# Opening and closing turns of a 64-batch GNN and attention kernel: steps listed by hand, weights in 21 loads, and matmuls of zeros ahead of the first products

## The chip, the cores and the metric

The kernel runs on one core of a Trainium2 chip. A core has a matrix engine (TensorE, PE in the profile), a vector engine (VectorE, DVE), a scalar engine (ScalarE, ACT), a general engine (GpSimd, POOL) and a queue engine (SyncE, SP) that here only starts DMA transfers; sixteen DMA engines do the moving. Each engine works through its own instructions in the order in which they were written into its queue, and waits where one needs a result of another engine. The metric is the device time of one execution in microseconds (us); lower is better. A time is given as the median of the runs with the lowest and the highest.

## The reference

Two layers over 64 batches of 256 tokens with 512 features, all in float32. Layer 0 averages neighbours with a weighted adjacency matrix and applies one linear layer; layer 1 is attention of 8 heads whose scores are multiplied by twice the adjacency matrix. Both end in a residual and a normalisation.

```python
# layer 0
deg = jnp.sum(adj, axis=-1, keepdims=True)
agg = jnp.einsum('bij,bjf->bif', adj, x) / jnp.maximum(deg, EPS)
cat = jnp.concatenate([x, agg], axis=2)
out = jax.nn.relu(jnp.einsum('bnf,of->bno', cat, W))      # W is 512 x 1024
x = _layernorm(x + out, axis=-1)
# layer 1
q, k, v = proj(Wq, bq), proj(Wk, bk), proj(Wv, bv)        # each 512 x 512, 8 heads of 64
scores = jnp.einsum('bhqd,bhkd->bhqk', q, k) * SCALE
scores = scores * (adj + adj)[:, None, :, :]
attn = jax.nn.softmax(scores, axis=-1)
ctx = jnp.einsum('bhqk,bhkd->bhqd', attn, v)
x = _layernorm(x + (jnp.einsum('bse,fe->bsf', ctx, Wo) + bo), axis=-1)
```

## The kernel before

**Products.** Each of the four large products of a batch (L: layer 0 on x, 1024 columns; Q: queries and keys together; V; O: the output projection) is done as a two-by-two block product with seven multiplications in place of eight. So there are steps L1 to L7, Q1 to Q7, V1 to V7 and O1 to O7 (lines 320 to 356 and 370 to 417). The weights are kept as seven blocks: four that are loaded (B11, T3, B21, B22 before they are combined) and sums of them, T1 to T4, made by `sum_blocks` (line 171). The other operand has four sums as well: xS1 to xS4 from the turned x (`xT0`, `xT1`), yS from the turned layer-0 result (`x1T`), cS from the attention's context; they are made by POOL on line 288. Results leave PSUM by a copy (`Lk5`, `Qk4` and so on; ACT, for O on DVE) or by an addition to what is there (`Lj3`, `Vj2`; DVE, line 328).

**The other steps of a batch.** `Dzx` and `Dza` load x and adj in a form that DVE can turn (xT, aT), `Dx` and `Dadj` load them by rows. `AY0` and `AY1` multiply the adjacency with the layer-0 product (line 442), `AYa`, `AYb`, `AYp`, `AYn` add, normalise and write layer 0's result into x (ACT, line 434). `Dway` writes it to DRAM, `Dz1` reads it back turned by blocks, `x1T` finishes the turn on DVE (line 482). Then Q and V. `Sa` to `Sd` are the score products of four pairs of heads (line 517), `ma`.. the mask on DVE, `Ma`.. the row maxima, `ea`/`fa`.. the exponentials on ACT (line 546), `ra`.. reciprocals, `na`.. the scaling on ACT (line 563), `Ta`.. a turn on DVE (line 570), `Dwa` and `Dsa`.. a round trip through DRAM (lines 575 and 584). `C0a`, `C0b`, `C1a`, `C1b` multiply the attention of pairs a, b, c, d with v (line 600), `c0` and `c1` copy the context (ACT, line 616). `Drest` fetches layer 0's result again and `bo` adds the bias to it on POOL (line 496), O's keeping steps add it (line 415), `lb`, `lp`, `ln` normalise (lines 422 to 434) and `Dout` stores.

**Order.** The order on every queue is written by hand. `PLAN` lists each step once with an offset: a turn of the loop on line 660 takes steps of several batches, `Sa+0` of batch i, `L5+2` of batch i+2, `O1-1` of batch i-1. The loop runs i from -6 to B+5 (B is 64), and a step is left out where its batch does not exist. So the first and last turns are the plan with holes in it. Ahead of the loop stand the loads for the first batches and the weights: `first_weights` (line 179; W0 half on the SP queue, half on the ACT queue, then wq, the biases, and the turn and sums of batch 0), and `more_loads` (line 191; wk, wv, wo on SP). `load_blocks` issues one DMA for each block and each group of 32 partitions, 64 KB each, for wo one for each block: 84 in all. Inside the loop, `later_weights` (line 196) stands ahead of V2 of batch 0 and scales the query weights and sums wqk on DVE and wv on POOL in one piece; `last_weights` (line 203) stands ahead of `bo` of batch 0 and folds the value bias into the output bias with eight matmuls (`p_bv`, line 210).

**DMA issue.** The completion semaphores of the DMAs are eight, used in turn, so a queue issues its next DMA only when the one that used the same semaphore before has landed.

Of the kernel before, what the change touches and what calls it, by code (L numbers as in the profile page):

```python
# [7 lines left out]
F32 = mybir.dt.float32  # L8
AF = mybir.ActivationFunctionType
ALU = mybir.AluOpType  # L10
AX = mybir.AxisListType

P = 128
# [3 lines left out]

PLAN = """  # L20
    Sa+0 AYn1+1
    Sb+0 ma+0 ln0-2 Dway+1
# [34 lines left out]
    Q4+1 lb1-1 Vk4+1 lp0-1 AYn0+2 Qj3+1 lp1-1 AYb1+2  # L57
    Q2+1 Qk4+1 AYp1+2 ln1-1 Qj2+1
"""


@with_exitstack
def kernel(
# [12 lines left out]
    bo: bass.AP,  # L76
    out: bass.AP,
):

# [18 lines left out]
    nc = tc.nc  # L100
    B, N, F = x.shape
    H = 8
    D = F // H
    NT = N // P
    FC = F // P
    G = F // 2
    L = 32
    A = P // L
    R = 2 * NT

    QSCALE = 2.0 * D ** -0.5

    const = ctx.enter_context(tc.tile_pool(name="const", bufs=1))
# [15 lines left out]
    def bank(name, b):  # L129
        return tile_of(name, b, [P, F], banks, "ps")  # L130
# [12 lines left out]
    def groups():  # L143
        return ((a, slice(a * L, (a + 1) * L)) for a in range(A))
# [4 lines left out]

    B11, B21, B22, T1, T2, T3, T4 = range(7)
    w0 = const.tile([P, 7, 2, 2, G], F32, name="w0")
    wqk = const.tile([P, 7, 2, 2, G], F32, name="wqk")
    wv = const.tile([P, 7, 2, G], F32, name="wv")
    wo = const.tile([P, 7, 2, G], F32, name="wo")

    def load_blocks(queue, dst, dram, swapped=False, natural=False):

        for blk, kh, nh in ((B11, 0, 0), (T3, 0, 1), (B21, 1, 0), (B22, 1, 1)):  # L160
            nh ^= swapped
            cols = dram[:, nh * G : (nh + 1) * G]
            if natural:
                rows = cols.rearrange("(c p) o -> p c o", p=P)
                queue.dma_start(out=dst(slice(None), blk), in_=rows[:, 2 * kh : 2 * kh + 2])
                continue
            rows = cols.rearrange("(a c l) o -> a l c o", a=A, c=FC)
            for a, part in groups():
                queue.dma_start(out=dst(part, blk), in_=rows[a, :, 2 * kh : 2 * kh + 2])

    def sum_blocks(engine, w):
        for dst, a, b in ((T1, T3, B11), (T2, B22, T1), (T3, B22, T3), (T4, B21, T2)):
            engine.tensor_tensor(w[:, dst], w[:, a], w[:, b], ALU.subtract)  # L173

    bqk = const.tile([P, 2, FC], F32, name="bqk")
    bvT = const.tile([P, FC], F32, name="bvT")
    bo_sb = const.tile([P, F], F32, name="bo_sb")

    def first_weights():
        load_blocks(nc.scalar, lambda p, k: w0[p, k, :, 1], w0t[F:])  # L180
        load_blocks(nc.sync, lambda p, k: w0[p, k, :, 0], w0t[:F])
        load_blocks(nc.scalar, lambda p, k: wqk[p, k, :, 0], wqt, swapped=True)
        nc.scalar.dma_start(out=bqk[:, 0], in_=bq)
        nc.scalar.dma_start(out=bqk[:, 1], in_=bk)
        nc.scalar.dma_start(out=bvT, in_=bv.rearrange("o (c p) -> p (o c)", p=P))
        nc.scalar.dma_start(out=bo_sb, in_=bo.to_broadcast([P, F]))
        for name in ("xT0", "xT1", "xS1", "xS2", "xS4", "xS3"):
            run(name, 0)
        sum_blocks(nc.vector, w0.rearrange("p k c m o -> p k (c m o)"))

    def more_loads():
        load_blocks(nc.sync, lambda p, k: wqk[p, k, :, 1], wkt, swapped=True)
        load_blocks(nc.sync, lambda p, k: wv[p, k], wvt)
        load_blocks(nc.sync, lambda p, k: wo[p, k], wot, natural=True)

    def later_weights():
        nc.vector.tensor_scalar(bqk[:, 0], bqk[:, 0], QSCALE, None, ALU.mult)
        for k in (B11, T3, B21, B22):
            nc.vector.tensor_scalar(wqk[:, k, :, 0], wqk[:, k, :, 0], QSCALE, None, ALU.mult)
        sum_blocks(nc.vector, wqk.rearrange("p k c m o -> p k (c m o)"))  # L200
        sum_blocks(nc.gpsimd, wv.rearrange("p k c o -> p k (c o)"))

    def last_weights():

        bv_all = tile_of("bv_all", 0, [P, NT, F], tag="h1")[:, 0].rearrange("p (c q) -> p c q", c=FC)
        nc.vector.tensor_copy(bv_all, bvT.unsqueeze(2).to_broadcast([P, FC, P]))
        ps = bank("p_bv", 0)
        for n, blocks in enumerate(((B11, B21), (T3, B22))):
            for c in range(FC):
                nc.tensor.matmul(  # L210
                    ps[:, n * G : (n + 1) * G],
                    lhsT=bv_all[:, c],
                    rhs=wo[:, blocks[c // 2], c % 2],
                    start=(c == 0),
                    stop=(c == FC - 1),
                )
        nc.vector.tensor_tensor(bo_sb, ps, bo_sb, ALU.add)
        sum_blocks(nc.gpsimd, wo.rearrange("p k c o -> p k (c o)"))


    def turned_rows(dram, a, width):
# [83 lines left out]
    WEIGHTS = {1: B11, 2: B21, 3: B22, 4: T4, 5: T1, 6: T2, 7: T3}  # L305
# [38 lines left out]
    def right_weights(left, w, width):  # L344
        def multiply(k, b, ps, first):
            for c in range(2):
                nc.tensor.matmul(  # L347
                    ps[:, :width],
                    lhsT=left(k, b, c),
                    rhs=w[:, WEIGHTS[k], c],  # L350
                    start=first and c == 0,
                    stop=True,
                    skip_group_check=True,
                )

        return multiply
# [13 lines left out]
    def multiply_q(k, b, ps, first):  # L370
        for m in range(2):
            for j in range(2):
                for c in range(2):
                    nc.tensor.matmul(  # L374
                        ps.rearrange("p (m j q) -> p m j q", m=2, j=2)[:, m, j],
                        lhsT=wqk[:, WEIGHTS[k], c, m, j * P : (j + 1) * P],
                        rhs=left_y(k, b, c),
                        start=first and m == j == c == 0,
                        stop=True,
                        skip_group_check=True,  # L380
                    )
# [4 lines left out]
    def keep_q(b, ps, t, n):  # L386
        for m in range(2):
            for j in range(2):
# [6 lines left out]
                )  # L395

    winograd("Q", multiply_q, keep_q, part_q)

    def part_v(b, t, n):
# [239 lines left out]
            nc.sync.dma_start(out=token_rows(out[b], a), in_=held["h1", b][part])  # L639


    plan = [(name[:-2], int(name[-2:])) for name in PLAN.split()]
    done = set()

    def run(name, b):
        if 0 <= b < B and (name, b) not in done:
            done.add((name, b))
            steps[name](b)

    with tc.manual_schedule():  # L650
        run("Dzx", 0)
        first_weights()
        run("Dza", 0)
        run("Dadj", 0)
        run("Dx", 0)
        run("Dadj", 1)
        run("Dadj", 2)
        run("Dzx", 1)
        more_loads()
        for i in range(-6, B + 6):  # L660
            for name, ahead in plan:
                if name == "V2" and i + ahead == 0:
                    later_weights()
                if name == "bo" and i + ahead == 0:
                    last_weights()
                run(name, i + ahead)


# [34 lines left out]
```

## Time and profile before

| what | value |
|---|---|
| median of 3 runs | 3129.31 us (3128.94 to 3130.68) |
| time of the profiled execution | 3130.71 us |
| its span, first to last instruction | 3128.9 us |
| instructions | 51253 |
| PE busy | 3062.6 us |
| DVE, ACT, POOL busy | 2082.1, 1712.2, 974.2 us |
| DMA | 513.35 MB, mean 164 GB/s |
| mean granted TensorE clock | 0.992 |

The span leaves out 1.8 us of the profiled execution's own time, and the median of the other runs lies 0.4 us above the span. A group in the profile is one line of the program, one engine, one operation and the tiles it writes and reads; a row of the timeline gives start, length, engine, line, operation, written tile, read tiles, shape and count, and in brackets how long the engine stood idle before it and what ended that. `PEld` rows are the weight loads of the matrix engine, which run beside its multiplications. A float32 matmul appears as two rows of the count: L's step of two matmuls is `x4`.

### The profile page before, as it was taken

To read this page: it belongs to the slowest core of one execution; us is meant where nothing else is said; L and a number is where in the kernel's file an instruction comes from. 1 tells how busy PE (TensorE), PEld (TensorE's weight loads), DVE (VectorE), ACT (ScalarE), POOL (GpSimd) and SP (SyncE) were. 2 spreads that over 40 slices of the span, in tenths; PEclk is the share of its full clock that TensorE was granted. 3 is DMA by queue.
4 is the path that set the end of the run, shared out by engine and by line. 5 is a ranking of instruction groups with operands and counts; after the bars stand their busy time and mean duration, and the time that the engine had idled before them with its cause. 6 is when DMAs were issued, how large, how long until landed. Compare 5 with 4: busy or idle time off the path is not lost. (4 is left out here: it accounts for less than half of the span.)

```text
span 3128.9 us, 51253 instructions
## 1 busy us (share of the span) xinstructions
PE 3062.6 (98%) x17168; PEld 2265.9 (72%) x17168; DVE 2082.1 (67%) x3599; ACT 1712.2 (55%) x4993; POOL 974.2 (31%) x1677
## 2 busy tenths in 40 slices
PE   5999999999999999999999999999999999999996
PEld 2776777777777777777767777777777777777674
DVE  4666666666766766666666666667667666666664
ACT  1555556555555555555555565555555555555654
POOL 2233323323233233233333233232332332333332
PEclk8999999999999999999999999999999999999998
DMA  6565655656656656656666567566566566566555
GB/s 148 125 165 159 182 160 157 185 154 160 182 156 161 182 153 171 173 151 182 165 159 182 154 163 186 155 159 181 157 161 182 152 172 173 151 182 165 159 155 141
DMA packets 498183, 513.35 MB, mean 164 GB/s; under 512 B 114816, under 2 KB 399488, under 8 KB 497920
## 3 DMA queue, kind: packets, MB, share of 16 engines
q1 hardware_dynamic: 494400, 507.70, 60.5%
q8 instruction: 137, 2.24, 0.3%
q10 hardware_dynamic: 3520, 2.37, 0.3%
q14 instruction: 126, 1.03, 0.1%
HBM read 308.55 MB, written 201.33 MB: 163 GB/s over the span
## 5 line engine op out<-in xcount | busy, mean ns | idle before, releaser
L390 ACT ACTIVATE qk<-Qa,bqk 128x128 f32<-128x128 f32 x768 | 218.6, 367 | 241.2 <-PE Qa L374 241.2
L363 ACT COPY oy<-La 128x512 f32<-128x512 f32 x192 | 112.3, 585 | 433.2 <-PE La L347 433.1
L428 POOL TENSOR_SCALAR mv<-mv 128x1 f32<-128x1 f32 x256 | 55.7, 217 | 935.1 <-DVE mv L423 919.4
L405 ACT COPY v<-Va 128x256 f32<-128x256 f32 x192 | 70.1, 365 | 365.3 <-PE Va L347 365.3
L347 PE MATMUL Lc<-w,xS 128*128 128x512 f32 x512 | 249.8, 611 | 14.5 <-DVE w L173 14.5
L374 PEld LDWEIGHTS Qa<-x1T,wqk 128*128 128x128 f32 x2048 | 248.8, 192 | 6.6
L374 PEld LDWEIGHTS Qa<-yS,wqk 128*128 128x128 f32 x2048 | 248.8, 192 | 6.6
L288 POOL TENSOR_TENSOR cS<-cT 128x256 f32<-128x256 f32 x128 | 93.2, 729 | 509.2 <-ACT cT L616 509.2
L374 PE MATMUL Qc<-yS,wqk 128*128 128x128 f32 x2048 | 249.6, 275 | 0.0
L374 PE MATMUL Qa<-x1T,wqk 128*128 128x128 f32 x2048 | 249.3, 275 | 0.0
L374 PE MATMUL Qa<-yS,wqk 128*128 128x128 f32 x2048 | 249.3, 275 | 0.0
L347 PE MATMUL La<-w,xS 128*128 128x512 f32 x512 | 243.3, 598 | 5.4 <-POOL xS L288 3.0
L347 PE MATMUL La<-w,xT 128*128 128x512 f32 x512 | 241.6, 594 | 0.8 <-DVE oy L328 0.8
L374 PEld LDWEIGHTS Qc<-yS,wqk 128*128 128x128 f32 x2048 | 239.0, 192 | 0.0
L442 PE MATMUL AY<-oy,aT 128*128 128x512 f32 x512 | 233.0, 598 | 4.6 <-DVE oy L328 4.6
L415 DVE TENSOR_TENSOR h<-Oa,rest 128x256 f32<-128x256 f32 x192 | 81.5, 425 | 220.3 <-PE Oa L347 200.7
L328 DVE TENSOR_TENSOR oy<-Lc,oy 128x512 f32<-128x512 f32 x64 | 44.2, 691 | 276.0 <-PE Lc L347 271.0
L288 POOL TENSOR_TENSOR yS<-x1T 128x256 f32<-128x256 f32 x128 | 93.3, 729 | 350.2 <-DVE x1T L482 350.2
L347 PEld LDWEIGHTS Lc<-w,xS 128*128 128x128 f32 x512 | 93.2, 192 | 132.3 <-issue 108.8
L288 POOL TENSOR_TENSOR xS<-xT 128x256 f32<-128x256 f32 x128 | 93.4, 730 | 299.1 <-DVE xT L253 299.1
L454 DVE SCALAR_TENSOR_TENSOR oy<-AY,deg,oy 128x512 f32<-128x512 f32 x128 | 94.9, 741 | 135.7 <-PE AY L442 135.7
L546 ACT ACTIVATE sa<-sa,nmaxa 128x256 f32<-128x256 f32 x256 | 127.0, 497 | 99.8 <-DVE nmaxa L540 99.8
(119 smaller groups left out, 7274.4 us busy)
## 6 DMA issues: line engine op xcount, KB each, us to landing
zx<-in_x_dram SPq DMA_DIRECT2D x256, 128.0 KB, 3.6
x<-in_x_dram SPq DMA_DIRECT2D x256, 128.0 KB, 3.4
way<-x SPq DMA_DIRECT2D x64, 512.0 KB, 3.2
z<-way SPq DMA_DIRECT2D x256, 128.0 KB, 3.0
wsa<-sa SPq DMA_DIRECT2D x64, 512.0 KB, 2.6
wsb<-sb SPq DMA_DIRECT2D x64, 512.0 KB, 3.0
sTa<-wsa SPq DMA_DIRECT2D x256, 128.0 KB, 3.6
wsc<-sc SPq DMA_DIRECT2D x64, 512.0 KB, 2.7
```

What stands on the lines that cost most here:

```text
L288: nc.gpsimd.tensor_tensor(part_of(s, b, [P, 4, 2, P])[:, k], left(b), right(b), op)
L328: nc.vector.tensor_tensor(dst, ps.rearrange(shape, **sizes), dst, ALU.add)
L347: nc.tensor.matmul(ps[:, :width], lhsT=left(k, b, c), rhs=w[:, WEIGHTS[k], c], start=first and c == 0, stop=True, skip_group_check=True,)
L363: nc.scalar.copy(part_l(b, t, n), ps.rearrange("p (m o) -> p m o", m=2))
L374: nc.tensor.matmul(ps.rearrange("p (m j q) -> p m j q", m=2, j=2)[:, m, j], lhsT=wqk[:, WEIGHTS[k], c, m, j * P : (j + 1) * P], rhs=left_y ...
L390: nc.scalar.activation(part_q(b, t, n)[:, m, j], ps.rearrange("p (m j q) -> p m j q", m=2, j=2)[:, m, j], AF.Identity, bias=bqk[:, m, c : ...
L405: nc.scalar.copy(part_v(b, t, n), ps[:, :G])
L415: nc.vector.tensor_tensor(part_o(b, t, n), ps[:, :G], rest, ALU.add)
L428: nc.gpsimd.tensor_scalar(mv[:, 1:2], mv[:, 1:2], LN_EPS, None, ALU.add)
L442: nc.tensor.matmul(ps, lhsT=held["aT", b][:, j, t], rhs=held["oy", b][:, 1, j], start=(j == 0), stop=(j == NT - 1),)
L454: nc.vector.scalar_tensor_tensor(h, held[f"AY{t}", b], rdeg, h, ALU.mult, ALU.add)
L546: nc.scalar.activation(rows(b)[:, r], rows(b)[:, r], AF.Exp, bias=of("nmax", b)[:, r : r + 1], accum_out=of("total", b)[:, r : r + 1],)
```

## The change

`START` and `END` are two new lists with a batch behind each step. `START` replaces everything ahead of the loop and the loop's turns up to i = 2; the batch number is the true one. `END` replaces the turns from i = 60 on; its number counts from the end, 1 is batch 63. The loop keeps `PLAN` for i from 3 to 59. The guard against running a step twice is gone.

Weights are loaded whole: one DMA takes 32 partitions of all four blocks, 256 KB; wo is one DMA of 1 MB. That is 8 DMAs for W0, 8 for wq and wk, 4 for wv and 1 for wo, 21 in place of 84. The biases move from the ACT queue to the SP queue. A block is now a strided part of the loaded tile: the two halves (x part and neighbour part) of an L weight lie 2048 elements apart, where they were adjacent; the sums T1, T2, T4 have a tile of their own, T3 is formed in place. Each sum is a step of its own (`W0s1` to `W0s4`, and so on); those of wo stay on POOL, those of wv too. The scaling of the query weights (`WqS`) is one instruction on ACT, of 2048 elements a partition, in place of four on DVE of 512.

`warm` is new: DVE writes zeros into the place of the W0 sums, and PE multiplies them 12 times (128x512, float32).

```diff
+FIRST_TURN = 3
+LAST_TURNS = 4
+START = """
+    warm:0 Dzx:0 W0:0 xT1:0 xT0:0 xS1:0 xS3:0 Dx:0 xS2:0 Dza:0 xS4:0 Dadj:0 Dzx:1 L1:0 W0s1:0 W0s2:0 Dadj:1
+    L2:0 Lk1:0 W0s3:0 Wo:0 L6:0 W0s4:0 deg:0 L5:0 Lk6:0 aT:0 Wb:0 L7:0 Lk5:0 L3:0 Lj7:0 Dza:1 L4:0 Wq:0
+    Lj3:0 Lj2:0 Lk4:0 xT1:1 AY1:0 xT0:1 xS1:1 AY0:0 xS3:1 AYa1:0 L5:1 AYb1:0 AYa0:0 AYp1:0 L1:1 Dzx:2
+    xS2:1 AYn1:0 AYb0:0 L2:1 bv1:0 AYp0:0 aT:1 xS4:1 bv2:0 AYn0:0 Lk1:1 Dway:0 Wv:0 Lk5:1 Lj2:1 L6:1
+    Wos1:0 Lk6:1 WqS:0 L7:1 Dz1:0 L3:1 Lj7:1 Wqs1:0 Dx:1 L4:1 Lj3:1 Dadj:2 Wvs1:0 Wqs2:0 Lk4:1 Wos2:0
+    Dza:2 AY1:1 x1T:0 AY0:1 xT1:2 yS1:0 deg:1 yS2:0 Q1:0 Wqs4:0 Wvs3:0 AYa1:1 Wvs2:0 V1:0 Qk1:0 Q5:0
...
+"""
+END = """
...
+    Ok4:4 Sa:2 Dsb:3 ma:2 V5:2 fb:2 V1:2 Dsd:3 Ma:2 Vk5:2 V2:2 Vk1:2 lb1:4 fa:2 Sd:2 Drest:3 Dz1:1 md:2
...
+    c1:3 Mc:2 Q5:1 Qk1:1 yS2:1 Dwb:2 cS1:3 Q6:1 cS2:3 Qk5:1 cS3:3 fc:2 yS4:1 O1:3 cS4:3 Q3:1 Qk6:1 Ok1:3
+    Ta:2 yS3:1 ec:2 Q7:1 Qj3:1 Dwa:2 ed:2 rc:2 O6:3 Qj7:1 nc:2 Ok6:3 Sb:1 rd:2 mb:1 O7:3 nd:2 Sa:1 Dsa:2
+    Mb:1 O5:3 Tc:2 Q4:1 fb:1 Ok5:3 Dwc:2 Oj7:3 ma:1 Qk4:1 O4:3 Ma:1 eb:1 Q2:1 Td:2 ea:1 O2:3 Ok4:3 Dwd:2
+    Qj2:1 fa:1 C0a:2 Drest:2 Dsc:2 rb:1 Sc:1 nb:1 ra:1 Sd:1 Dsb:2 mc:1 O3:3 na:1 lb1:3 Dsd:2 Mc:1 lp1:3
+    Oj3:3 fc:1 Oj2:3 V1:1 lb0:3 ec:1 C1a:2 Ta:1 lp0:3 C0b:2 bo:2 ln1:3 md:1 Dwa:1 V5:1 ln0:3 rc:1 Md:1
+    C1b:2 nc:1 Dout:3 ed:1 Tc:1 fd:1 Tb:1 Dwc:1 Dsa:1 c0:2 rd:1 c1:2 Dwb:1 nd:1 O1:2 cS1:2 O2:2 cS2:2
+    Ok1:2 cS3:2 O6:2 Vk1:1 Td:1 Vk5:1 cS4:2 O5:2 Oj2:2 Dwd:1 V6:1 Ok6:2 Dsc:1 Ok5:2 O7:2 Vk6:1 V7:1
+    Dsb:1 Oj7:2 O4:2 O3:2 Ok4:2 lb1:2 Drest:1 V3:1 Dsd:1 Vj7:1 lp1:2 Oj3:2 V4:1 lb0:2 V2:1 Vk4:1 lp0:2
+    ln1:2 Vj2:1 Vj3:1 ln0:2 C0a:1 Dout:2 C1a:1 C0b:1 bo:1 C1b:1 c0:1 c1:1 O2:1 cS1:1 O1:1 cS2:1 O5:1
+    cS4:1 Ok1:1 O6:1 cS3:1 Ok5:1 O3:1 Ok6:1 Oj2:1 O7:1 Oj3:1 Oj7:1 lb0:1 O4:1 lp0:1 Ok4:1 lb1:1 ln0:1
+    lp1:1 ln1:1 Dout:1
+"""
...
+    def weights(name, engine, parts, flip=0):
+        raw = const.tile([P, parts, FC, 2, G], F32, name=name)
+        sums = const.tile([P, 3, parts, 2, G], F32, name=f"{name}_sums")
+        def block(k):
+            if k >= T1:
+                return sums[:, k - T1]
+            return raw[:, :, k // 2 * 2 : k // 2 * 2 + 2, k % 2 ^ flip]
...
+    def load_weights(queue, raw, part, dram):
+        rows = dram.rearrange("(a c l) (n o) -> a l c n o", a=A, c=FC, n=2)
+        for a, p in groups():
+            queue.dma_start(out=raw[p, part], in_=rows[a])
+    @step("W0")
+    def _(_):
+        load_weights(nc.scalar, w0_raw, 1, w0t[F:])
+        load_weights(nc.sync, w0_raw, 0, w0t[:F])
...
+    @step("WqS")
+    def _(_):
+        nc.scalar.mul(bqk[:, 0], bqk[:, 0], QSCALE)
+        nc.scalar.mul(wqk_raw[:, 0], wqk_raw[:, 0], QSCALE)
...
+    @step("warm")
+    def _(b):
+        zeros = w0(T1)[:, 0].rearrange("p c o -> p (c o)")
+        nc.vector.memset(zeros, 0.0)
+        ps = bank("p_warm", b)
+        for _ in range(12):
+            nc.tensor.matmul(ps, lhsT=zeros[:, :P], rhs=zeros, start=True, stop=True)
...
                 nc.tensor.matmul(
-                    ps[:, :width],
+                    ps[:, :width].rearrange("p (m o) -> p m o", o=G),
                     lhsT=left(k, b, c),
-                    rhs=w[:, WEIGHTS[k], c],
+                    rhs=w(WEIGHTS[k])[:, :, c],
...
-        for i in range(-6, B + 6):
-            for name, ahead in plan:
-                if name == "V2" and i + ahead == 0:
-                    later_weights()
-                if name == "bo" and i + ahead == 0:
-                    last_weights()
+        for name, b in listed(START):
+            run(name, b)
+        for i in range(FIRST_TURN, B - LAST_TURNS):
+            for name, ahead in turn:
                 run(name, i + ahead)
+        for name, b in listed(END):
+            run(name, B - b)
```

## The prediction

> **What bounds the kernel now.** I read the page's shares and slices first.
>
> ```profile
> PE 3062.6 (98%) x17168; PEld 2265.9 (72%) x17168; DVE 2082.1 (67%) x3599; ACT 1712.2 (55%) x4993; POOL 974.2 (31%) x1677
> ...
> PE   5999999999999999999999999999999999999996
> ...
> PEclk8999999999999999999999999999999999999998
> ```
>
> TensorE sets the time, and only the first and the last of 40 slices (78 us each) have holes. The steady turns leave nothing to win. PE's timeline gives the price of one, from the first context matmul of one batch to that of the next:
>
> ```profile
> 189.07 1.08 PE L600 MATMUL pc<-sTa,v 128*64 128x256 f32 x8
> ...
> 2991.37 1.08 PE L600 MATMUL pc<-sTa,v 128*64 128x256 f32 x8
> ...
> 3038.87 1.08 PE L600 MATMUL pc<-sTa,v 128*64 128x256 f32 x8
> ```
>
> The last two stand 47.50 us apart, and 189.07 to 3038.87 is 60 turns of 47.50. So 64 batches are 3040.0 us of matmuls, p_bv (148.70 to 152.15) 3.45 more: 3043.5 us. The span is 3128.9, so 85.4 us are lost. Where? Starts of neighbouring steps give 1.72 us for an L step and for each of AY0, AY1, 1.78 for a Q step, 0.865 for a V, O, S or C step; ahead of 189.07 stand batch 0, batches 1 and 2 each without C and O, L and AY of batch 3, and p_bv: 47.5 + 2 x 38.0 + 15.5 + 3.45 = 142.4 us. The start loses 46.7, the end the other 38.7. The waits of PE name most of it:
>
> ```profile
> PE Lc L347 <- DVE w L173: 14.5, 1, 14.5
> PE Vb L347 <- issue: 10.1, 1, 10.1
> PE pc L600 <- DMA sTc<-wsc: 8.6, 1, 8.6
> PE Oa L347 <- DVE h L415: 5.1, 5, 1.4
> PE AY L442 <- DVE oy L328: 4.6, 1, 4.6
> PE Oa L347 <- DVE h L328: 3.9, 2, 3.4
> PE La L347 <- POOL xS L288: 3.0, 1, 3.0
> ```
>
> And these rows of the timelines say why:
>
> ```profile
> 14.53 3.75 PE L347 MATMUL Lc<-w,xS 128*128 128x512 f32 x4 [14.53 <-DVE w L173]
> 18.07 2.03 PE L347 MATMUL La<-w,xT 128*128 128x512 f32 x4
> ...
> 24.22 2.79 PE L347 MATMUL La<-w,xS 128*128 128x512 f32 x4 [2.39 <-issue]
> ...
> 62.86 2.05 PE L347 MATMUL Vb<-wv,x1T 128*128 128x256 f32 x4 [10.06 <-issue]
> ```
> ```profile
> 48.40 0.41 SPq L469 DMA_DIRECT2D way<-x  x1
> ```
> ```profile
> 63.50 4.63 DVE L199 TENSOR_SCALAR wqk<-wqk 128x512 f32<-128x512 f32 x4
> 68.06 5.82 DVE L173 TENSOR_TENSOR wqk<-wqk 128x1024 f32<-128x1024 f32 x4
> ```
>
> The same four passes take 3.75 us after a pause and 1.72 in the stream: PE starts at half clock and needs about 3.5 us to be granted the full one, a loss of 1.75. It happens at 14.5, 24.2, 45.7, 62.9 and 74.5: 8.8 of the start's 46.7. V2 of batch 0 waits for the round trip of layer 0's result, whose store was issued at 48.40 because 36 weight loads, 0.47 us each, stood ahead of it on SP (30.92 to 48.29; ACT had finished x at 45.0). The 10.45 us of scaling and summing on DVE then hold the join that AY waits for.
>
> **The change, part by part.**
>
> *First matmul.* SP and ACT issue 4 W0 loads each instead of 16. Removed: 24 issues, and the wait for eight semaphores with only 64 KB behind each. The data stays: zx 0.52 MB and W0 2.1 MB ahead of the first product, which now is L1 and needs all of W0 but no sum. Rates: 215 to 226 GB/s while zx runs (2 to 6 us), 292 where 256 KB pieces run (48 to 53 us). From 2.2 us: 2.4 + 7.2 = 11.8, with a landing 13. Bounds: 11 (everything at the 334 GB/s of 52 to 54 us) and 16.5 (the 174 of the first 13 us).
>
> *Zeros.* 12 matmuls of two passes: 0.86 us each at full clock, 1.72 at half. The memset, never seen here, lies between POOL's 0.10 us and the 0.69 of a DVE row of 512 elements; I take the latter, so PE starts at 1.5 us. 3.5 us at half clock are two matmuls, ten more 8.6: over at 13.6. Bounds 11.8 (full clock at once) and 22.1 (never). So L1 of batch 0 starts at about 14.0, at full clock. W0's sums overwrite the zeros, hence wait for the last of them, and take DVE 4 x 1.2 us; the first two are needed by L6 two L steps later (3.4 us), so they are covered; without that cover, 2.4 us.
>
> [...]
>
> *To the end of AY of batch 1.* PE has 2 x 15.5 + 3.45 = 34.4 us, since p_bv now stands here. Waits: the last join and copy ahead of AY, 0.9 in all (DVE 0.69, ACT 0.58). PE is ready for Q1 of batch 0 at 49.3.
>
> *Round trip of layer 0.* Behind W0 on SP stand 41 issues up to Dway: x, za, adj, zx of batch 1, adj, wo, four biases, za, wq and wk, zx of batch 2; 6.0 MB. wq moved here from ACT, wv behind Dway; 41 x 0.47 = 19 us of issuing, so the data decides: at 230 GB/s (between 203 at 53 to 62 us and 292) 26 us, to 39. Then way, wv and z1, 2.1 MB, at 240: 48; landing 1, x1T 1.25 (row at 61.51): 50.3. A wait of 1 to 2 us; I take 2. Bounds: 0 (all at 292: done at 44), and 12 with a clock loss (6.0 MB at 164, the rate of 23 to 48 us). The scaling on ACT (2048 elements; four copies of 512 are 2.3) and four DVE sums (5.8) now lie in pieces between joins; I add 1.5 for waits on these and yS.
>
> Start: 14.0 + 0.9 + 2 + 1.5 = 18.4 against 46.7.
>
> *Steady turns.* 57 instead of all; the list is unchanged. L's moving operand comes in two runs of 256 elements. The S and C matmuls already read runs of 32 (the rearranged qk and sT), and C's eight passes take 0.865 us, two side by side, as do V's four of one run. So nothing; bounds 0 and the rival below.
>
> *End.* O steps of batches 61 and 62, V of 63 and C of 62 now stand where PE waited 8.6 us for sTc. What decides is ACT. From Sb of 63 to O1 of 62 PE has five O, three S, four C, two V steps (12.1 us) and two Q (3.6): 15.7. ACT must do in that time, ahead of the copies c0, c1 that O1 needs: 16 exponentials (0.49 a piece, 7.9), the scaling of 62 d and of 63 a, b, c (1.6 each, 6.5), a Q copy and two norms (2.6): 17.0, and it can't start c, d before their masks and maxima (2.5 us of DVE each pair). I take 4.5 us of waiting; bounds 0 and 9. The last sT: scaling d, turn 1.2, then five transfers of 0.52 MB at 231 GB/s (the row pattern of 3092 to 3106: 3.1 MB in 13.5 us) make it 2 late (0 to 6). The same bunching for batch 62, 2; x1T of 63, whose store waits behind transfers of 61, 1. After the last context matmul the old chain took 3108.5 to 3128.9, 20.4 us. The POOL addition of `rest` leaves it (DVE waited for it from 3111.2 to 3113.2), O3 fills a wait, one norm goes ahead of the last join (0.8 of DVE, 1.3 of POOL, 0.8 of ACT fewer): 20.4 - 3.9 = 16.5, of which 6.05 are O's own matmuls. End: 4.5 + 2 + 2 + 1 + 10.4 = 19.9 against 38.7.
>
> *Sum.* 3043.5 + 18.4 + 19.9 = 3081.8 of span. The median of the runs was 0.4 above the profiled span (that execution itself 1.8): 3082 us, 47 below.
>
> **The rivals.**
>
> 1. *The DMA queue ends last at the start.* 8 MB stand ahead of x1T in one queue. For it: loads ran at 164 GB/s; against: their 64 KB pieces held them at the rate of issue, 0.47 us each. +10 with a clock loss: 3094.
> 2. *The end gives little.* ACT's 14.3 us of exponentials and scaling a batch and the DRAM round trip are as long as before and beside the tail's 3.9 none to half of the 14.9 of waits comes back: 3089 to 3097.
> 3. *The zeros run too long.* All at half clock they end at 22.1, 8 late: 3090. Against: the row at 18.07.
> 4. *Better:* neither ACT nor DMA is late. Waits of 3 in place of 14: 3071.
> 5. *Slower: the split moving operand.* If a second run cost a tenth of an L pass (0.43), 0.043 x 28 passes x 64 = 77 us: 3159. It decides from 26 ns a pass (47 us over 1792 passes). Against: the runs of 32 above.
>
> **How the numbers follow.** Forecast 0.60, its own range 3074 to 3091; rivals 0.13, 0.10, 0.05, 0.09, 0.03. 3069 to 3097 leaves out the slower rival, the first and second together, and a part of the fourth. Below 0.2% (6 us) a measurement can't tell a change: same 0.01, which takes 23 to 30 ns a pass in rival 5 or all waits at their far bounds. Faster 0.96, slower 0.03.
>
> **What would show it.** Right: the first real matmul at 13 to 15 us with 1.72 us for four passes; Q1 of batch 0 at 49 to 52; 47.50 between turns; waits at the end on the context copies (ACT) and on the last sT, 5 to 10 us in all; from last context matmul to the end 16 to 17. Wrong: a turn other than 47.50, or a wait on x1T over 6 us. The prediction falls if a wait repeats in every turn.

## The result, and the profile after

The changed kernel takes 3096.47 us in the median of 4 runs (3093.03 to 3098.72), the kernel before 3129.99 on the same chip (3128.94 to 3131.17): ratio 0.9892, interval 0.9875 to 0.9909. It is 33 us faster, where 47 were forecast. The time is 14 us above the forecast of 3082 and outside the forecast's own range (3074 to 3091); it lies in the wide range of 3069 to 3097 by 0.5 us, because that range takes in rival 2. The profiled execution took 3098.72 with a span of 3096.9; every run lists 1.8 us more than its span, so the 0.4 with which the prediction went from span to median was 1.4 too small.

The page's shares and slices of the changed kernel, as shown of before:

```profile
PE 3070.2 (99%) x17192; PEld 2269.5 (73%) x17192; DVE 2079.4 (67%) x3595; ACT 1713.3 (55%) x4995; POOL 978.8 (32%) x1677
...
PE   9999999999999999999999999999999999999997
...
PEclk9999999999999999999999999999999999999998
```

PE's first slice went from 5 to 9, the last only from 6 to 7. Part of the first 9 are the 24 matmul rows of zeros, which do no work, so a full slice is no proof of a gain: the waits tell more. PE's largest waits after (total, count, longest):

```profile
PE Qa L472 <- DVE x1T L580: 5.7, 2, 3.5
PE pc L698 <- DMA sTc<-wsc: 2.5, 1, 2.5
PE pc L698 <- DMA sTd<-wsd: 2.4, 1, 2.4
PE La L445 <- DMA W<-in_w0t_dram: 2.2, 1, 2.2
PE p_warm L316 <- DVE W_sums L313: 1.4, 1, 1.4
PE pc L698 <- DMA sTb<-wsb: 1.3, 1, 1.3
```

The waits of 14.5, 10.1 and 8.6 us of before are gone; no new one is over 3.5. PE's timeline, the start and two steady turns:

```profile
1.44 12.38 PE L316 MATMUL p_warm<-W_sums 128*128 128x512 f32 x24 [1.44 <-DVE W_sums L313]
15.98 1.96 PE L445 MATMUL La<-W,xT 128*128 128x512 f32 x4 [2.16 <-DMA W<-in_w0t_dram]
...
53.86 2.05 PE L472 MATMUL Qa<-x1T,Wq 128*128 128x128 f32 x16 [2.18 <-DVE x1T L580]
...
206.87 1.13 PE L615 MATMUL sca<-qk 64*128 64x256 f32 x8
254.36 1.14 PE L615 MATMUL sca<-qk 64*128 64x256 f32 x8
```

The zeros end at 13.8, as forecast, but W0 is there only at 15.98 (forecast 14.0). Q of batch 0 waits 2.18 us for x1T (forecast 2). A turn of the loop is 47.49 us, the old one (47.50) within the rounding: no cost of the split moving operand shows.

The rows of the closing list:

```profile
3022.09 3.42 PE L472 MATMUL Qa<-x1T,Wq 128*128 128x128 f32 x16 [3.50 <-DVE x1T L580]
...
3051.53 1.08 PE L698 MATMUL pc<-sTc,v 128*64 128x256 f32 x8 [2.47 <-DMA sTc<-wsc]
...
3053.95 1.97 PE L698 MATMUL pc<-sTb,v 128*64 128x256 f32 x8 [1.34 <-DMA sTb<-wsb]
...
3059.76 1.26 PE L445 MATMUL Oa<-Wo,cT 128*128 128x256 f32 x4
...
3077.09 1.98 PE L698 MATMUL pc<-sTd,v 128*64 128x256 f32 x8 [2.41 <-DMA sTd<-wsd]
```

The row at 3059.76 is O1 of batch 62, which the forecast had waiting 4.5 us for ACT's copies: it has no wait.

Read the length as well as the bracket: the same eight passes take 1.08 us in the first C row and 1.97 in the next, because the granted clock fell to half. The table of stretches says so (start:end, length, PE busy, PEld, DVE, ACT, POOL, granted clock, DMA share, GB/s):

```profile
3054.00:3060.00 6.00, 6.00 (x21) 2.96 (x22) 3.10 (x4) 3.79 (x14) 0.88 (x1) 0.50 1.02 334
3077.00:3083.00 6.00, 5.22 (x16) 3.40 (x17) 0.00 (x0) 0.58 (x1) 3.46 (x5) 0.51 0.02 6
```

So a late sT cost here its wait and then, by an estimate from these clocks, up to 3 us more in the 6 us at 0.50 and 0.51 that follow.

**Where the time lies.** The loop's 57 turns run from 206.87 to 2914.4 (57 times 47.50 later). What `START` and `END` list comes, by the prediction's prices of a step, to 184.3 and 147.9 us; scaled by 47.50 over 46.97 (a turn as it is, and by those prices) these are 186.4 and 149.6. So the start loses 20.5 us (46.7 before, forecast 18.4) and the end 3096.9 - 2914.4 - 149.6 = 32.9 (38.7 before, forecast 19.9). Nearly all that is missing is missing at the end.

**Why sT is late.** The SP queue of the changed kernel at its end:

```profile
3005.43 0.44 SPq L567 DMA_DIRECT2D way<-x  x1
...
3011.74 2.02 SPq L573 DMA_DIRECT2D z<-way  x4
...
3020.98 0.37 SPq L673 DMA_DIRECT2D wsb<-sb  x1
...
3043.82 0.34 SPq L673 DMA_DIRECT2D wsd<-sd  x1
...
3044.73 2.24 SPq L682 DMA_DIRECT2D sTc<-wsc  x4
3047.01 2.43 SPq L682 DMA_DIRECT2D sTb<-wsb  x4
```

ACT finished x of batch 63 at 2997.9, its store `way` is issued at 3005.43, behind transfers of batch 61. `wsb` of batch 62 is stored at 3020.98 and read back as sTb only at 3047.01, 26 us later: `sTb`, and sTc whose store was issued at 3039.46, stand in the list behind the store of `wsd`, which waits for the turn of d on DVE (it ends at 3043.8). What is late there is a place in a queue, not data.

### The profile page after: what moved, and what is told of

The parts are those of the page before. It is cut to its first block, busy times and chain, and to the rows that moved or that the text cites. A ratio compares the mean times of both kernels' runs of the same rounds, so it can differ in the third digit from the quotient of the medians.

```text
span 3096.9 us, 51211 instructions
## 1 busy us (share of the span) xinstructions
PE 3070.2 (99%) x17192; PEld 2269.5 (73%) x17192; DVE 2079.4 (67%) x3595; ACT 1713.3 (55%) x4995; POOL 978.8 (32%) x1677
## 4 chain that ended last, share of the span: by engine, by line
PE 96%; DMA 3%; DVE 1%; SPq 0%; issue 0%; POOL 0%; ACT 0%; POOLq 0%; DVEq 0%
PE Qa L472 15%; PE La L445 14%; PE Qc L472 7%; PE pc L698 7%; PE Lc L445 7%; PE Oa L445 7%; PE AY L540 7%; PE Va L445 7%; PE Qb L472 4%; PE Vc L445 4%; PE Oc L445 3%; PE Lb L445 3%; PE sca L615 2%; PE scb L615 2%; PE Ob L445 2%; PE scc L615 2%
## 5 line engine op out<-in xcount | busy, mean ns | idle before, releaser
L594 POOL TENSOR_TENSOR rest<-rest,bo_sb 128x512 f32<-128x512 f32 x128 | 159.9, 1272 | 28.1 <-DMA rest<-way 28.1
L540 PEld LDWEIGHTS AY<-oy,aT 128*128 128x128 f32 x512 | 97.0, 190 | 96.7 <-issue 91.9
L527 POOL TENSOR_TENSOR mv<-mv,neg_half 128x1 f32<-128x1 f32 x256 | 143.9, 562 | 21.3
L472 PEld LDWEIGHTS Qa<-x1T,Wq 128*128 128x128 f32 x1024 | 125.6, 194 | 11.3 <-DVE x1T L580 6.9
L472 PE MATMUL Qa<-x1T,Wq 128*128 128x128 f32 x1024 | 126.2, 277 | 5.7 <-DVE x1T L580 5.7
L644 ACT ACTIVATE sb<-sb,nmaxb 128x256 f32<-128x256 f32 x256 | 128.8, 511 | 3.6 <-DMA za<-in_adj_dram 2.2
L644 ACT ACTIVATE sd<-sd,nmaxd 128x256 f32<-128x256 f32 x256 | 127.3, 501 | 1.7 <-DVE nmaxd L638 1.7
L644 ACT ACTIVATE sc<-sc,nmaxc 128x256 f32<-128x256 f32 x256 | 127.3, 501 | 1.4 <-DVE nmaxc L638 1.4
L472 PEld LDWEIGHTS Qa<-x1T,Wq_sums 128*128 128x128 f32 x1024 | 124.4, 192 | 3.9 <-issue 0.8
L472 PEld LDWEIGHTS Qa<-yS,Wq 128*128 128x128 f32 x1024 | 124.2, 192 | 4.0 <-issue 0.9
```

The costliest lines, as they stand in the source:

```text
L472: nc.tensor.matmul(ps.rearrange("p (m j q) -> p m j q", m=2, j=2)[:, m, j], lhsT=wqk(WEIGHTS[k])[:, m, c, j * P : (j + 1) * P], rhs=left_y ...
L527: nc.gpsimd.tensor_tensor(mv[:, 1:2], mv[:, 1:2], neg_half, ALU.pow)
L540: nc.tensor.matmul(ps, lhsT=held["aT", b][:, j, t], rhs=held["oy", b][:, 1, j], start=(j == 0), stop=(j == NT - 1),)
L594: nc.gpsimd.tensor_tensor(rest, rest, bo_sb, ALU.add)
L644: nc.scalar.activation(rows(b)[:, r], rows(b)[:, r], AF.Exp, bias=of("nmax", b)[:, r : r + 1], accum_out=of("total", b)[:, r : r + 1],)
```

## The experiments

All ratios are against the kernel before on the same chip. The experiments ran in four groups (e1 to e4; e5 to e8; e9 to e11; e12), not all on one chip: the kernel before took 3130.7, 3130.6, 3130.8 and 3130.3 us in them, the changed kernel, run again in the second, 3096.09 (3094.02 to 3098.03). Differences below 2 us between experiments mean little.

### e1: without the zeros

```diff
 START
-    warm:0 Dzx:0 W0:0 xT1:0
+    Dzx:0 W0:0 xT1:0
```

> The changed kernel without the zeros' memset and twelve matmuls; all else as it is. Theory 1 (the zeros hide the half-clock start): W0's landing still ends the first wait, so L1 of batch 0 starts at 15.5 to 16.0 us, but its first four passes take about 3.7 us, AY of batch 0 and the chain over x1T come 1.7 us later: 1.5 to 2.5 us slower than the changed kernel. Theory 2 (the start is bound by the DMA queue up to x1T): Q1 of batch 0 starts within 0.5 us of 53.9 and the time is the same within 0.5. Theory 3 (the zeros hold up W0's sums): faster by 0.5 to 1.

Measured: 3093.66 (3090.0 to 3094.19), ratio 0.9877, interval 0.9864 to 0.9891. PE's timeline:

```profile
15.05 3.75 PE L445 MATMUL La<-W,xT 128*128 128x512 f32 x4 [15.05 <-DMA W<-in_w0t_dram]
...
52.63 2.00 PE L472 MATMUL Qa<-x1T,Wq 128*128 128x128 f32 x16
```

The first four passes take 3.75 us, as in the kernel before, where those in the stream take 1.88. But Q of batch 0 has no wait in brackets now: PE comes there as x1T does, and in the changed kernel the 1.8 us that the zeros saved were spent waiting for x1T. While x1T is last, the zeros hide nothing that lasts. The time is not above the changed kernel's but 2.8 us below it, which no theory had. Of the 5.5 us between the two profiled spans (3091.4 and 3096.9) 1.3 lie ahead of the loop's first scores (205.59 against 206.87), with W0 landing at 15.05 against 15.98; the rest lies in the end, whose list is the same in both, and where e5, the changed kernel again, is 1.8 us shorter too: the end scatters by such amounts without any edit.

### e2: seven steps of the SP queue moved in the closing list

```diff
 END
-    AYn1:1 Td:3
+    AYn1:1 Dway:1 Td:3
-    eb:2 Dway:1 Ok4:4
+    eb:2 Ok4:4
-    Dsb:3 ma:2
+    Dsb:3 Dz1:1 ma:2
-    Drest:3 Dz1:1 md:2
+    Drest:3 md:2
-    Qj3:1 Dwa:2
+    Qj3:1 Dsb:2 Dwa:2
-    Ok4:3 Dwd:2
+    Ok4:3 Dsc:2 Dwd:2
-    Drest:2 Dsc:2 rb:1
+    rb:1
-    Sd:1 Dsb:2 mc:1
+    Sd:1 mc:1
-    Dsd:2 Mc:1
+    Dsd:2 Drest:2 Mc:1
-    Oj2:2 Dwd:1 V6:1 Ok6:2 Dsc:1 Ok5:2
+    Oj2:2 Dsc:1 Dwd:1 V6:1 Ok6:2 Ok5:2
-    Drest:1 V3:1 Dsd:1 Vj7:1
+    V3:1 Dsd:1 Drest:1 Vj7:1
```

> The changed kernel with seven steps moved in END, all of them transfers on SP: way of 63 right after its norm, z1 of 63 ahead of sTd of 61, sTb of 62 ahead of the store of pair a, sTc of 62 and 63 ahead of the store of pair d, rest of 62 and 63 behind sTd. Theory 1 (what the end lost beyond the prediction lies in the order of the SP queue): the waits on x1T of 63 (3.5), sTc and sTb of 62 (2.5, 1.3) and sTd of 63 (2.4) shrink to under 3 us together and the half-clock stretches after them go: 8 to 16 us faster, 3081 to 3089. Theory 2 (ACT's exponentials and scalings bound the end, as the prediction had it): the waits only change their names, at most 3 us faster.

Measured: 3089.5 (3087.8 to 3091.51), ratio 0.9867, interval 0.9853 to 0.988: 6 to 7 us below the changed kernel, a little less than the 8 to 16 of theory 1, since a wait that had been hidden came out. SP and PE at the end:

```profile
3019.97 0.38 SPq L672 DMA_DIRECT2D wsb<-sb  x1
3023.20 1.73 SPq L681 DMA_DIRECT2D sTb<-wsb  x4
...
3034.20 0.34 SPq L672 DMA_DIRECT2D wsc<-sc  x1
...
3036.86 1.73 SPq L681 DMA_DIRECT2D sTc<-wsc  x4
```

```profile
3002.41 1.03 PE L444 MATMUL Oa<-Wo_sums,cT 128*128 128x256 f32 x4
3003.37 1.14 PE L614 MATMUL sca<-qk 64*128 64x256 f32 x8
3004.43 1.13 PE L444 MATMUL Vc<-Wv_sums,yS 128*128 128x256 f32 x4
...
3047.06 1.08 PE L697 MATMUL pc<-sTd,v 128*64 128x256 f32 x8 [0.33 <-DMA sTd<-wsd]
...
3052.46 1.82 PE L444 MATMUL Oa<-Wo,cT 128*128 128x256 f32 x4 [4.32 <-ACT cT L713]
```

sTb now follows its store by 3.2 us in place of 26. The waits on x1T of batch 63, sTc and sTb are gone and sTd's is 0.33. In their place O of batch 62 waits 4.32 us for ACT's context copies: this is the wait of 4.5 us that the prediction put there, with its reason (ACT has to do exponentials and scaling first; its rows from 3046.26 to 3052.89 show one gap, of 0.26 us). From the end of the last context matmul (3069.3) to the end of the span are 16.7 us, forecast 16.5. Start 20.1 and end 22.4 by the sum above (first scores of the loop at 206.51, span 3086.0): the end loses 10.5 less. The first three rows show a cost that stays: an S step that stands alone between steps of other kinds takes 1.06 us to the next start, the step ahead of it 0.96, where the price was 0.865.

### e3: the old closing turns

```diff
-        for i in range(FIRST_TURN, B - LAST_TURNS):
+        for i in range(FIRST_TURN, B + 6):
...
-        for name, b in listed(END):
-            run(name, B - b)
```

> START and all loads as in the changed kernel, END taken away: the plan's turns run out with holes, as in the kernel before. By the losses read from the two traces (38.7 at the end before, 32.5 after) it is 5 to 8 us slower than the changed kernel, 3102 to 3104. By the prediction's sizes (38.7 against 19.9) it would be 19 slower.

Measured: 3105.8 (3104.83 to 3107.94), ratio 0.9919. `END` is worth 9 to 10 us, half of the 18.8 that the prediction gave it and a little above what the experiment was expected to show. The waits of before are back: 9.5 us on sTc, 5.1 and 3.2 on h.

### e4: 84 loads of weights again, in the new order

```diff
-        for a, p in groups():
-            queue.dma_start(out=raw[p, part], in_=rows[a])
+        for nh, kh in ((0, 0), (1, 0), (0, 1), (1, 1)):
+            for a, p in groups():
+                k = slice(2 * kh, 2 * kh + 2)
+                queue.dma_start(out=raw[p, part, k, nh], in_=rows[a][:, k, nh])
...
-        nc.sync.dma_start(out=wo_raw[:, 0], in_=wot.rearrange("(c p) (n o) -> p c n o", p=P, n=2))
+        rows = wot.rearrange("(c p) (n o) -> p c n o", p=P, n=2)
+        for nh, kh in ((0, 0), (1, 0), (0, 1), (1, 1)):
+            k = slice(2 * kh, 2 * kh + 2)
+            nc.sync.dma_start(out=wo_raw[:, 0, k, nh], in_=rows[:, k, nh])
```

> The changed kernel with each weight load cut into four of 64 KB (wo: four of 256 KB), at the same places of the same queues: 84 loads. Theory 1 (fewer issues bring the weights earlier): 63 more issues at 0.47 us, so all of W0 lands at 18 or later, x1T of batch 0 is held by SP and Q1 of batch 0 starts at 60 to 66: 6 to 13 us slower. Theory 2 (the DMA engines are the limit at about 210 GB/s with either size): W0 within 1 us, Q1 within 3 us, at most 3 slower.

Measured: 3105.14 (3103.53 to 3106.09), ratio 0.9917: 9 us slower than the changed kernel. PE's timeline:

```profile
63.16 3.79 PE L477 MATMUL Qa<-x1T,Wq 128*128 128x128 f32 x16 [12.76 <-DVE x1T L585]
```

Q of batch 0 waits 12.76 us for x1T, and then takes 3.79 us, where the changed kernel's took 2.05. The issues are the cause that the prediction named for the wait of before: 16 for wk from 38.79 and 16 for wv from 49.09 stand around the store of x (48.64), and the z loads come at 57.14. But the first L step starts at 14.11 here, as soon as the zeros end: with smaller loads the blocks that it needs land earlier than with whole ones.

### e8: the old order of the start, with 21 loads and no zeros

`START` is the plan's own first turns, written out, with the weight loads and sums where the kernel before has them.

```diff
 START
-    warm:0 Dzx:0 W0:0 xT1:0 xT0:0 xS1:0 xS3:0 Dx:0 xS2:0 Dza:0 xS4:0 Dadj:0 Dzx:1 L1:0 W0s1:0 W0s2:0 Dadj:1
+    Dzx:0 W0:0 Wb:0 xT0:0 xT1:0 xS1:0 xS2:0 xS4:0 xS3:0 W0s1:0 W0s2:0 W0s3:0 W0s4:0 Dza:0 Dadj:0 Dx:0 Dadj:1
+    Dadj:2 Dzx:1 Wq:0 Wv:0 Wo:0 L5:0 L1:0 L2:0 Lk1:0 Lk5:0 aT:0 L6:0 L3:0 Lk6:0 Lj3:0 L7:0 Lj7:0 Lj2:0 L4:0
...
```

> END and the 21 loads as in the changed kernel, but START in the order of the kernel before: the plan's first turns with holes, all weight loads ahead of the loop, scaling and sums in one piece ahead of V2 of batch 0, no zeros. Theory 1 (the order of the steps is what the start won): way of batch 0 stands behind all weights and is issued at 42 to 46 us, V2 of batch 0 starts at 57 to 61, 22 to 27 us slower than the changed kernel, 3118 to 3124. Theory 2 (larger loads alone win the start): V2 of batch 0 before 52 and less than 10 us slower.

Measured: 3106.51 (3106.02 to 3110.72), ratio 0.9925, interval 0.9912 to 0.9937: 10 us slower than the changed kernel, where 22 to 27 were expected. PE's timeline:

```profile
17.08 3.75 PE L443 MATMUL Lc<-W_sums,xS 128*128 128x512 f32 x4 [17.08 <-DVE W_sums L237]
...
55.51 2.08 PE L443 MATMUL Vb<-Wv,x1T 128*128 128x256 f32 x4 [5.34 <-DVE x1T L578]
```

The first product needs the sums and comes later than in the kernel before (17.08 against 14.53), but V2 of batch 0 stands at 55.51 in place of 62.86. So the larger loads bring much of the start's gain in either order. With e3 and e4: the start's gain is some 24 us (33 less `END`'s 9). The new order with small loads (e4) keeps about 15 of them, the old order with large loads and without zeros (e8) about 14, so the two gains overlap by some 5.

### e5 and e6: the changed kernel again, and Wv behind z

e5 changes nothing; e6 issues Wv after z of batch 0.

```diff
 START
-    Dway:0 Wv:0 Lk5:1
+    Dway:0 Lk5:1
...
-    L7:1 Dz1:0 L3:1
+    L7:1 Dz1:0 Wv:0 L3:1
```

> The changed kernel itself, beside the others on one chip: 3093 to 3099, and L1 of batch 0 starting between 15 and 16 us. If the kernel without the zeros was truly faster, this is 2 to 3 us above 3093.7; if the zeros do nothing, its interval takes in 3093.7.

> The changed kernel with the four loads of Wv moved behind z1 of batch 0 in START. Theory 1 (the round trip of layer 0's result is held by what stands ahead of it on SP): z1 lands 3 to 5 us earlier, Q1 of batch 0 starts right after AY of batch 1, its wait of 2.2 us is gone: 1.5 to 2.5 us faster. Theory 2 (the DMA engines are full and the order of requests changes nothing): Q1 of batch 0 within 0.5 us, or V1 waits for Wv instead: the same.

Measured: e5 3096.09, ratio 0.9888 (0.9875 to 0.9902); Q of batch 0 at 54.00 after a wait of 2.67. e6 3097.35 (3095.86 to 3097.82), ratio 0.9891: the same. PE in e6:

```profile
53.97 1.10 PE L443 MATMUL Va<-Wv,x1T 128*128 128x256 f32 x4 [0.76 <-DMA Wv<-in_wvt_dram]
...
57.66 2.84 PE L470 MATMUL Qc<-yS,Wq_sums 128*128 128x128 f32 x16 [2.59 <-POOL yS L384]
```

Q comes at 51.26, 2.7 earlier than in e5, without a wait. The load of z is issued at 43.87, in the changed kernel at 44.18: what comes earlier is not the issue but the landing, now that Wv's 1 MB is not requested ahead of it. The wait then stands twice further on: V1 waits for Wv, and the next Q step for sums of y that POOL makes only after its first sum of Wv, which also waits for Wv. A step moved in one queue had a user in another queue with work behind it.

### e7: the context copies earlier

e2, and `c0` and `c1` of batch 62 ahead of exponentials and scaling of batch 63 on ACT.

```diff
 END
-    C1b:2 nc:1 Dout:3 ed:1
+    C1b:2 c0:2 nc:1 Dout:3 c1:2 ed:1
...
-    Dsa:1 c0:2 rd:1 c1:2 Dwb:1
+    Dsa:1 rd:1 Dwb:1
```

> The kernel with the seven moved transfers (end_queue) and, on ACT, the context copies c0 and c1 of batch 62 moved ahead of the scaling of pair c and the exponentials of pair d of batch 63. Theory 1 (the 4.3 us for which O1 of 62 waits are ACT's queue, not its work): the wait falls below 1 us, 3 to 5 us faster than end_queue, 3084.5 to 3086.5. Theory 2 (ACT has too much work at the end): the wait moves to the last sT or the last copies of the context, within 1 us of end_queue.

Measured: 3091.24 (3089.21 to 3093.68), ratio 0.9873 (0.986 to 0.9887): not better than e2. PE in e7:

```profile
3071.47 1.98 PE L697 MATMUL pc<-sTd,v 128*64 128x256 f32 x8 [3.00 <-DMA sTd<-wsd]
```

The wait of 4.3 us on the copies fell to 0.2; sTd of batch 63 is 3.0 late instead, with 1.98 us for the eight passes behind it (1.08 in e2), the second copy 0.95 and h 1.7. So the wait changed its name, as theory 2 had it. The rows of e2 and e7 can't be laid side by side as they stand: e7's start is 1.7 longer (first scores of the loop at 208.20 against 206.51). From there on ACT scales d of batch 63 0.3 later (3054.78 against 3052.79), sTd is issued 1.0 later (3065.52 against 3062.88), and the whole end is 3.4 longer. That ACT's amount of work sets this end is not shown.

### e9: e1 and e2 together

> The changed kernel without its zeros (as in the first experiment) and with the closing list of the second, in which seven DMA steps stand elsewhere. Theory 1 (start and end are lost independently, and both small gains are real): the two differences add, 2.8 and 7.0 us below 3096.5, so 3086 to 3087.5. Theory 2 (the 2.8 us without zeros was the scatter of the W0 landing, which differs by 1 us between runs): no better than the second experiment, 3088.5 to 3091, with the first Q step of batch 0 at 52 to 54 either way. In both the end after batch 62's products is as in the second experiment: one wait of about 4.3 us on the context copies of ACT.

The edits are those of e1 and e2. Measured: 3088.05 (3086.29 to 3088.24), ratio 0.9862 (0.9847 to 0.9876), between the two expectations. The first scores of batch 0 come at 71.40, 0.7 ahead of e2's, those of the loop at 205.88, 0.6 ahead. In both pairs (e1 and the changed kernel, e9 and e2) the kernel without zeros is the faster, by 2.8 and 1.5 us in the medians: a gain from the zeros is not shown in this order of loads, and a cost so small, between two groups of runs, isn't either.

### e10: the three queues of Wv together

e2, Wv later as in e6, and what waited then moved too: POOL's first sum of Wv behind the sums of y, and V1 behind two Q steps. The zeros stay.

```diff
 START
-    L4:1 Lj3:1 Dadj:2 Wvs1:0 Wqs2:0
+    L4:1 Lj3:1 Dadj:2 Wqs2:0
...
-    yS1:0 deg:1 yS2:0 Q1:0
+    yS1:0 deg:1 yS2:0 Wvs1:0 Q1:0
...
-    V1:0 Qk1:0 Q5:0
+    Qk1:0 Q5:0 V1:0
```

> The zeros stay, the closing list is that of the second experiment, and in the opening list the loads of Wv stand behind the load of z of batch 0 (as in the sixth experiment), and two steps more are moved that then waited for it: POOL's first sum of Wv behind the sums y of batch 0, and the first V step behind two Q steps. Theory 1 (x1T of batch 0 is late only because Wv's 1 MB stands ahead of z, and the sixth experiment gave this back through POOL's order): the first Q step of batch 0 at 51 to 51.5 without a wait, the first scores of batch 0 at 69.5 to 70.5 where the second experiment has 72.08, the whole 1.5 to 2.5 us below the second experiment, 3087 to 3088. Theory 2 (one later wait or another takes its place, since Wv's sums need Wv in any order): the scores of batch 0 at 72 to 74, the whole 3089 to 3092.

Measured: 3086.07 (3085.21 to 3088.26), ratio 0.9859, interval 0.9843 to 0.9875: the fastest of the kernels that compute the reference, 10 us below the changed one. PE:

```profile
51.50 1.95 PE L469 MATMUL Qa<-x1T,Wq 128*128 128x128 f32 x16
...
69.28 1.14 PE L612 MATMUL sca<-qk 64*128 64x256 f32 x8
```

No wait ahead of Q, none behind it, and the scores of batch 0 at 69.28, 2.8 ahead of e2. The start loses 17.2 us now (first scores of the loop at 203.59), the end 22.7 (span 3083.4).

### e11 and e12: W0 over 128 partitions

Both are made to see why W0 lands at 16 us. e11 is e2 with eight loads of W0 as large as before, each over all partitions. Its rows of W0 lie in the wrong partitions, so its output is not the reference's; it is there for its time alone:

```diff
-        load_weights(nc.scalar, w0_raw, 1, w0t[F:])
-        load_weights(nc.sync, w0_raw, 0, w0t[:F])
+        for queue, part in ((nc.scalar, 1), (nc.sync, 0)):
+            rows = w0t[part * F : (part + 1) * F].rearrange("(c p) (n o) -> p c n o", p=P, n=2)
+            for c in range(FC):
+                queue.dma_start(out=w0_raw[:, part, c], in_=rows[:, c])
```

> The second experiment, with W0 loaded by eight transfers of the same 256 KB that each go to 128 partitions instead of 32; the rows of W0 then lie in other partitions, so the products of layer 0 are of other numbers, in the same time. Theory 1 (transfers into 32 partitions are what held the rate at 186 to 234 GB/s ahead of the first L step, against 311 GB/s for Wo's 128 partitions): W0 has landed by 13 us, the first L step starts when the zeros end, at 13.6 to 13.9, and Q of batch 0 is at most as early as its x1T, 51 to 53; the whole 0 to 2 us below the second experiment. Theory 2 (the rate is that of the first transfers after the start, whatever their shape): the first L step again at 15.0 to 16.2 with a wait of about 2 us on W0, and the same time as the second experiment within 1.5 us.

Measured: 3085.26 (3084.7 to 3085.58), ratio 0.9854, interval 0.9839 to 0.9869. Two stretches of the changed kernel and the same of e11 (the last three columns are clock, DMA share, GB/s):

```profile
6.00:8.00 2.00, 2.00 (x6) 0.88 (x5) 0.00 (x0) 0.35 (x1) 0.00 (x0) 1.00 1.15 200
8.00:10.00 2.00, 2.00 (x6) 0.95 (x5) 0.37 (x1) 0.00 (x0) 0.00 (x0) 1.00 1.13 210
```

```profile
6.00:8.00 2.00, 2.00 (x7) 0.80 (x6) 0.00 (x0) 0.00 (x0) 0.00 (x0) 1.00 1.13 306
8.00:10.00 2.00, 2.00 (x6) 0.95 (x5) 1.23 (x2) 0.00 (x0) 0.43 (x1) 1.00 1.02 366
```

The DMA engines are as busy in both, and move half as much again to three quarters more in e11. e11 changes two things at once, the partitions and the way a transfer's rows go to them (128 rows on end in both, but in the changed kernel each of 32 partitions takes four that lie 32 rows apart, in e11 each of 128 takes one), and the runs do not part them. All stretches of the changed kernel from 2 to 16 us show 186 to 234 GB/s. The first L step starts at 13.58, when the zeros end, 2.2 ahead of e2, and the scores of batch 0 come at 69.30 against 72.08. Here the zeros do their work: its four passes take 1.88 us.

e12 is e10 with such loads and every row in its own partition, so that it computes the reference:

```diff
+            rows = w0t[part * F : (part + 1) * F].rearrange("(a c l) o -> c a l o", a=A, c=FC)
+            for c in range(FC):
+                queue.dma_start(out=w0_raw[:, part, c].rearrange("p n o -> p (n o)"), in_=rows[c])
```

> The tenth experiment (closing list of the second, Wv and its first sum later, zeros kept) with W0 loaded by eight transfers of 256 KB that go to 128 partitions each, as in the eleventh, but with every row in the partition where it belongs, so the output is the reference's. Theory 1 (the two gains lie one behind the other on the path of TensorE, so they add): the first L step at 13.6, 2.4 earlier than in the tenth; Q of batch 0 35.5 later, at 49.1, without a wait on x1T; the first scores of batch 0 at 66.8 to 67.2; the whole 3083 to 3084.5. Theory 2 (x1T of batch 0 is bound by its own data again once TensorE comes 2.4 earlier): a wait of 1 to 2 us ahead of Q of batch 0, the first scores at 68 to 69.3, the whole 3085 to 3086.5.

Measured: 3100.98 (3099.94 to 3104.01), ratio 0.9909, interval 0.9895 to 0.9922: 15 us slower than e10, which neither theory had. One stretch, and PE's first L rows:

```profile
8.00:10.00 2.00, 2.00 (x6) 0.95 (x5) 0.00 (x0) 0.00 (x0) 0.00 (x0) 1.00 0.28 92
```

```profile
18.80 2.05 PE L444 MATMUL La<-W,xT 128*128 128x512 f32 x2 [3.75 <-DMA W<-in_w0t_dram]
22.83 2.08 PE L444 MATMUL La<-W,xT 128*128 128x512 f32 x2 [1.99 <-DMA W<-in_w0t_dram]
```

The DMA engines are busy for a share of 0.28 of their time, at 92 GB/s; 0.28 of sixteen is the work of four or five, but no view here lists the engines one by one. W0 comes in drops, each pair of passes waits for one (3.75, 1.99, 2.11 and 0.81 us), and the granted clock is 0.73 from 16 to 20 us and 0.50 from 20 to 34. The one difference to e11's loads is the order of rows in DRAM: 128 rows on end there, here four groups of 32 rows that lie 128 rows apart. Why that order keeps the share at 0.28 is not shown. A W0 that is laid out in DRAM beforehand, so that e11's loads compute the reference, was not tried.

## Why the prediction was right and where it was wrong

- *Direction and steady turns: right.* The turn is 47.49 to 47.50, the slower rival (a split moving operand) did not come. Of the other signs that it named for being right only the wait on the last sT came (2.41): the first matmul stands at 15.98 (13 to 15), Q of batch 0 at 53.86 (49 to 52), O of 62 does not wait for the context copies, and from the last context matmul to the end it is 17.8 us (16 to 17).
- *Zeros: right in length, not in worth.* They end at 13.8 (13.6). As the prediction had x1T late by 2 us anyway, its own sum should have said that a faster first matmul only lengthens that wait; e1 shows it. Only where W0 comes earlier (e11, and e4 with its first product at 14.11) do the zeros stand directly ahead of a product.
- *First matmul: 2 us too early.* The term "2.4 + 7.2" divided 2.1 MB by 292 GB/s, the rate of other transfers of 256 KB. The changed kernel has 200 and 210 GB/s there, and e11, with 306 and 366, shows that the form of the loads makes the difference. The size of a transfer was compared, its form was not.
- *Round trip of layer 0: right in the difference.* 2.18 us of waiting against 2; but PE is ready at 51.7 (49.3) and x1T there at 53.9 (50.3), and that two errors of 2.4 and 3.6 us leave so small a rest is luck. Its reason, data and not issue, holds with the larger loads; e4 shows the issue bound of before with 12.76 us. e10 shows which data: Wv's 1 MB ahead of z.
- *Start in all:* 20.5 against 18.4.
- *End: the step that failed.* "What decides is ACT" named one bound and forgot a second, the order of issue on SP. The prediction charged x1T of 63 with 1 us, the transfers of batch 62 (sTc and sTb) with 2 and the last sT with 2, by transfer rates. Measured were 3.50, 2.47 and 1.34, and 2.41 us of waits, and behind them about 1.7, 3.0 and 2.9 us lost at a granted clock of 0.57, 0.50 and 0.51 (3022 to 3026, 3054 to 3060, 3077 to 3083): 17 us in place of these 5, while ACT's 4.5 did not show at all, hidden behind them. The view was there: the two lists show each DMA step's place among the others, but the prediction went through SP's queue step by step at the start only. e2 is the proof: with seven steps of that queue moved, the end loses 22.4 (forecast 19.9), the ACT wait appears at 4.32, the tail is 16.7. With the queue in order the forecast's end was 2.5 us off, but in part by luck: its 5 us for transfers measured 0.3, and in their place stand 1.8 us in the three O steps behind the ACT wait (1.61, 1.71 and 1.06 us from start to start against 0.865) and about 4 that it had at nothing, S and C steps that stand singly between others (an estimate from the starts of e2's rows against 0.865; some 30 places).
- *Rival 2, "the end gives little",* had the place right and 3089 to 3097 for the time, for another reason (ACT's work and the round trip as long as before). e2 speaks against that reason as the whole of it, since SP's order alone gives 7 of the missing 13 us back in the medians, and 10.5 in the profiles. That 3096.47 lies within the wide range owes to this rival's numbers and is luck as far as its reason goes.
- Half clock: the prediction charged it at the start only. At the end of the changed kernel it comes three times with work under it, from 3022.5, 3053.2 and 3077.1.
- From span to median 1.4 us too little.

## What to carry to other kernels

When a list of steps is written by hand for the ramps of a pipeline, walk each DMA queue on its own: beside every load write when its data is ready, and look at what stands ahead of it and what that waits for. A step moved on one queue pulls its users on the others with it (e6 against e10), so move them together or the wait only changes its name. Before paying for a warm-up, see whether what comes behind it is late anyway.

## What was not expected of the hardware

- A pause lowers the clock at lengths that do not separate: after 2.16 and 2.18 us at the start the next passes took 1.96 and 2.05 us, nearly the full rate (1.88 and 1.95); after 2.41 (sTd) they took 1.98 in place of 1.08, and after 2.47 (sTc) 1.08, with half clock only from the following step on. In e6 2.59 us were followed by 2.84 in place of 1.95. What tells the four in the changed kernel apart is where they fall. In its trace the granted clock changes at 3022.5, 3025.9, 3053.2, 3060.1, 3077.1, 3084.0 and 3090.8, which is 3.41, 27.3, 6.83, 17.1, 6.83 and 6.83 us apart, all whole multiples of 3.41. Counted off in steps of 3.41 us from these changes, one in which PE was busy for only 0.42, 1.08 or 1.00 us (from 3019.09, 3049.81, 3073.71) is followed by half clock, while the steps with the pauses of 2.16 and 2.18, which straddle an edge, still hold 1.87, 2.19 and 2.46 us of work (from 11.95, 49.49, 52.91) and are not. Counted off in the same way in the kernel before, steps with 0.28, 1.02 and 1.53 us of work (from 52.51, 21.79, 3083.55) are followed by half clock, those with 1.89 and 2.04 (from 3046.00, 3080.14) are not; no step at full clock had between 1.53 and 1.87 in these two traces. Up to 18 us the trace of before shows 1.00 throughout, even where four passes took 3.75. In these rows a pause of 2.4 us cost up to 3 us behind it where it fell into one such step, and since an order of steps doesn't fix where that is, it has to be priced as a risk.
- Three ways of writing W0 in transfers of the same 256 KB: into 32 partitions 200 to 210 GB/s (the changed kernel), into 128 from rows on end 306 to 366 (e11; other loads among them in all three), into 128 from four groups of rows 92 (e12).
